# Block 1 of a gated cross-attention network: loads in parts, and products of weights inside the steps

## The chip, the cores and the metric

The kernel runs on one core of one Trainium2 chip. The metric is the device time of one execution in microseconds (us). TensorE (PE) multiplies matrices, VectorE (DVE) does elementwise work and reductions, ScalarE (ACT) exponentials and copies, GpSimd (POOL) some elementwise work and indirect transfers; SyncE (SP) issues most of the transfers.

## The reference, cut to what matters

Four blocks, each a gated cross-attention and a gated feed-forward part, work on x of 16 sequences by 128 tokens by 256 in float32. The change touches the first attention alone:

```
x = x + tanh(g_xattn[0]) * L0_xattn(layernorm(x), ctx, mask, Wq, Wk, Wv, Wo)

L0_xattn: 16 query heads, 8 key/value heads, head size 128
  q = (xn @ Wq)    k = (ctx @ Wk)    v = (ctx @ Wv)      # k, v repeated for two heads each
  attn = softmax(q k^T / sqrt(128), masked)
  out  = concat_heads(attn v) @ Wo
```

x is (16, 128, 256), ctx (16, 128, 128), Wq (256, 2048), Wk and Wv (128, 1024), Wo (2048, 256).

## The kernel before, in words

`Net.__init__` loads x in four parts of four sequences on SP's queue, and on ScalarE's queue the constants, the gates and the whole of the context in two layouts (`ctxT`, `ctx`, 1 MB each). The tiles stay in SBUF for the whole kernel.

`xattn0` never forms q, k and v. `products0` multiplies weights first. For each head h the query product is `wm[h] = Wq_h Wk_h^T / sqrt(128)` (256 by 128: two matmuls into a buffer of the PSUM tag `mm`, evicted by ScalarE, L578 and L581), and the value product is `wn[h] = Wv_h Wo_h` (128 by 256: one matmul into `mm`, evicted by ScalarE into the place of Wo's head, L562 and L563). Before the change all 16 query products and then all 16 value products come ahead of the steps. Four loads on SP's queue feed them: `wa` (WqT, 2 MB), `wc` (WkT, 0.5 MB), `wd` (WvT, 0.5 MB), `wb` (Wo, 2 MB).

The steps run over 64 units. `place(n)` takes a unit as a group g of four sequences (n // 16), a group of four heads hq (n // 4 % 4) and a sequence i of the group (n % 4). Step n issues, in the order of the text:

- `scores(n)`: four matmuls of `qT` with `ctxT` into PSUM tag `sc` (L620); VectorE adds the mask bias (s, L624), takes maxima (L527), subtracts them (e, L528); ScalarE takes the exponential (L531); VectorE sums and inverts (L538 to L542); GpSimd multiplies (L543)
- `queries(n // 4 + 1, n % 4)`: two matmuls of one head's `wm` with `xnT`, 512 columns wide, into `mm` (L609), copied to `qT` by ScalarE (L613). Four of them, one a step, make the next unit group's `qT`
- `turn(n - 1)`: four transposes (L516) and ScalarE's copy to `pT` (L518)
- `values(n - 2)`: one matmul with `ctx` (L634), ScalarE's copy to `aT` (L636)
- `project(n - 3)`: four matmuls with `wn` (L643), added to x by VectorE (L410)
- the layernorm of the next group of sequences, spread over a few steps (`norm_steps`: statistics at step 6, rows at 7 and 8, turns at 8 and 9 for the second group), and mask biases.

Ahead of step 0 come the layernorm of group 0, its mask bias and four `queries`. The order is written out by hand for TensorE, VectorE, ScalarE and GpSimd:

```python
with self.tc.manual_schedule(engines={ET.PE, ET.DVE, ET.Activation, ET.Pool}):
```

Inside it, each of these engines gets its instructions in the order of the program. SP is not in that list. PSUM tags have fixed numbers of buffers in this block: `sc` 2, `mm` 2, `tr` 2, `av` 1, `y` 1. At step 20 `empty_rows` starts filling buffers of the later routed parts with zeros on SP's queue. `ffn0` follows and loads its weights into `wa` and `wd` again, once their last readers are done.

Of the kernel before, what the change touches and what calls it, by code (L numbers as in the profile page):

```python
# [28 lines left out]
P = 128  # L29
B = 16  # L30
S = 128
D = 256
# [257 lines left out]
class Net:  # L290
    def __init__(self, tc, ctx, t, out):
        self.tc, self.nc, self.t, self.out = tc, tc.nc, t, out
        nc = self.nc
        self.const = ctx.enter_context(tc.tile_pool(name="const", bufs=1))
        self.wpool = ctx.enter_context(tc.tile_pool(name="wpool", bufs=1))
        self.small = ctx.enter_context(tc.tile_pool(name="small", bufs=4))
        self.dram = ctx.enter_context(tc.tile_pool(name="dram", bufs=1, space=DRAM))
        c = self.const
        self.n = 0

        self.x = c.tile([P, B, D], F32, name="x_sb")
        for g in range(4):
            nc.sync.dma_start(
                self.x[:, 4 * g : 4 * g + 4, :],
                t["x"][4 * g : 4 * g + 4].rearrange("b s h -> s b h"),
            )
        self.cst = c.tile([P, C_END], F32, name="cst")
        nc.scalar.dma_start(self.cst, t["cst"])
        self.ident = self.cst[:, C_ID : C_ID + P]
        gates = c.tile([P, 8], F32, name="gates")  # L310
        nc.scalar.dma_start(gates, t["gates"].partition_broadcast(P))
        self.rows, self.results = {}, {}
        self.head = self.routed = None

        self.mark = None
        self.ctxT = c.tile([P, B, S], F32, name="ctxT")
        nc.scalar.dma_start(self.ctxT, t["ctxT"])
        self.ctx = c.tile([P, B, S], F32, name="ctx")
        nc.scalar.dma_start(self.ctx, t["ctx"])
        self.xnT = c.tile([P, 2, NT], F32, name="xnT")  # L320
        self.nhalf = c.tile([P, 32], F32, name="nhalf")
        nc.gpsimd.memset(self.nhalf, -0.5)
        self.ones = c.tile([P, P], F32, name="ones")
        nc.gpsimd.memset(self.ones, 1.0)
        self.tg = c.tile([P, 8], F32, name="tg")
        nc.scalar.activation(self.tg, gates, AF.Tanh)

    def empty_rows(self, names, pool, after=None):

# [226 lines left out]

    def value_products(self, bank, wvT, wo, kv_of):

        nc = self.nc
        for h in range(16):  # L560
            pr = self.psum(bank, [P, D])
            nc.tensor.matmul(pr, wvT[:, kv_of(h), :], wo[:, h, :], start=True, stop=True)  # L562
            nc.scalar.copy(wo[:, h, :], pr)  # L563
        return wo


    def products0(self, pool):

        nc, t = self.nc, self.t
        wqT = self.weight("wa", t["L0_WqT"].rearrange("(h p) n -> p h n", p=P), [P, 16, D])  # L570
        wkT = self.weight("wc", t["L0_WkT"].rearrange("(h p) n -> p h n", p=P), [P, 8, P])
        wvT = self.weight("wd", t["L0_WvT"].rearrange("(h p) n -> p h n", p=P), [P, 8, P])
        wo = self.weight("wb", t["L0_Wo"].rearrange("(h p) n -> p h n", p=P), [P, 16, D])
        wm = self.sb(pool, "wm", [P, 2, 16, P], bufs=1)
        for h in range(16):
            pr = self.psum("mm", [P, 2, P])
            for kk in range(2):
                nc.tensor.matmul(  # L578
                    pr[:, kk, :], wqT[:, h, kk * P : (kk + 1) * P], wkT[:, h // 2, :], start=True, stop=True
                )  # L580
            nc.scalar.activation(wm[:, :, h, :], pr, AF.Copy, scale=1.0 / math.sqrt(128.0))  # L581
        return wm, self.value_products("mm", wvT, wo, lambda h: h // 2)

    def xattn0(self):
        nc, t = self.nc, self.t
        with self.tc.tile_pool(name="a0", bufs=2) as pool, self.tc.tile_pool(name="a0s", bufs=3) as sp:
            wm, wn = self.products0(pool)
            mraw = self.sb(pool, "mraw", [P, B, S], mybir.dt.uint8, bufs=1)
            nc.scalar.dma_start(mraw, t["mask"].partition_broadcast(P))
            some = self.sb(pool, "some", [P, B], bufs=1)  # L590
            nc.vector.tensor_reduce(some, mraw, AX.X, ALU.max)
            qT, mb, e, pT, aT = {}, {}, {}, {}, {}

            def place(n):

                return n // 16, n // 4 % 4, n % 4

            def mask(g):
                mb[g] = self.sb(pool, "mb", [P, 4, S])
                nc.vector.tensor_scalar(mb[g], mraw[:, 4 * g : 4 * g + 4, :], -NEG, NEG, ALU.mult, ALU.add)  # L600

            def queries(m, j):

                g, hq = divmod(m, 4)
                if j == 0:
                    qT[m] = self.sb(pool, "qT", [P, 4, 512])
                mm = self.psum("mm", [P, 512])
                for kk in range(2):
                    nc.tensor.matmul(  # L609
                        mm, wm[:, kk, 4 * hq + j, :], self.xnT[:, kk, g * 512 : (g + 1) * 512],  # L610
                        start=kk == 0, stop=kk == 1,
                    )
                nc.scalar.copy(qT[m][:, j, :], mm)  # L613

            def scores(n):
                g, hq, i = place(n)
                b = 4 * g + i
                sc = self.psum("sc", [P, 4, S])
                for j in range(4):
                    nc.tensor.matmul(  # L620
                        sc[:, j, :], qT[n // 4][:, j, i * S : (i + 1) * S], self.ctxT[:, b, :], start=True, stop=True
                    )
                s = self.sb(sp, "s", [P, 4, S], bufs=2)
                nc.vector.tensor_tensor(s, sc, mb[g][:, i : i + 1, :].to_broadcast([P, 4, S]), ALU.add)  # L624
                e[n] = self.exp_rows(sp, s, 1.0)
                self.normalise(e[n], some[:, b : b + 1])

            def turn(n):
                pT[n] = self.transpose4(sp, e.pop(n))

            def values(n):
                g, hq, i = place(n)
                o = self.psum("av", [P, 4, S])
                nc.tensor.matmul(o, self.ctx[:, 4 * g + i, :], pT.pop(n), start=True, stop=True)  # L634
                aT[n] = self.sb(sp, "aT", [P, 4, S])
                nc.scalar.copy(aT[n], o)  # L636

            def project(n):
                g, hq, i = place(n)
                y = self.psum("y", [P, D])  # L640
                a = aT.pop(n)
                for j in range(4):
                    nc.tensor.matmul(y, a[:, j, :], wn[:, 4 * hq + j, :], start=j == 0, stop=j == 3)  # L643
                self.add_to_x(4 * g + i, y, self.tg[:, 0:1])

            ET = mybir.EngineType
            N = 4 * B
            norm = self.norm_steps(sp, -6, 16)
            with self.tc.manual_schedule(engines={ET.PE, ET.DVE, ET.Activation, ET.Pool}):
                self.layernorm(sp, groups=(0,))  # L650
                mask(0)
                for j in range(4):
                    queries(0, j)
                for n in range(N + 3):
                    if n < N:
                        scores(n)
                    if n + 4 < N:
                        queries(n // 4 + 1, n % 4)
                    if 0 <= n - 1 < N:
                        turn(n - 1)  # L660
                    if 0 <= n - 2 < N:
                        values(n - 2)
                    if 0 <= n - 3 < N:
                        project(n - 3)
                    for f in norm.get(n, ()):
                        f()
                    if n % 16 == 8 and n + 8 < N:
                        mask(n // 16 + 1)
                    if n == 20:
                        self.empty_rows(("f1", "f2"), self.const, aT[n - 2].rearrange("p h s -> p (h s)"))  # L670
# [947 lines left out]
```

## Time and profile before

| | |
|---|---|
| median of 3 runs | 2532.65 us (2532.24 to 2535.24) |
| the profiled execution | 2590.16 us, span from first to last instruction 2588.1 us |
| mean granted TensorE clock | 0.916 of full; 1.00 in the first 400 us |
| TensorE busy in the span | 80% |
| VectorE, ScalarE, GpSimd busy | 58%, 34%, 31% |
| DMA | 299.33 MB, mean 116 GB/s; 274 GB/s in the first 50 us |
| block 1's attention | from the start to about 415 us |

Times in the profile are those of one execution, taken by the hardware profiler; it was longer than the runs that gave the median. A line of the order of time gives the start, the duration, the engine, the line of the code, the operation with the tiles it writes and reads, the number of merged instructions, and in brackets how long the engine had been idle before it and what ended the wait. Durations of matmuls are modelled at their ends: consecutive ones overlap, so the time that one takes on TensorE is read from start to start. PEld is TensorE's loading of the stationary operand, which overlaps with matmuls.

### The profile page before, as it was taken

Reading aid. Unit: us, or ns where it says so; the run is one execution under the profiler, and the core shown is the slowest. Engines: PE = TensorE matmul, PEld = TensorE weight load, DVE = VectorE, ACT = ScalarE, POOL = GpSimd, SP = SyncE. Lnnn points to the kernel's source line nnn. Section 1 sums busy time; section 2 is a strip of 40 time slices with the busy share of each in tenths; the row PEclk is TensorE's granted clock in tenths of the full one; section 3 lists DMA queues with packets and bytes.
Section 4 is the critical chain, followed back from the end, with each engine's and each line's share of the span. In section 5 each row is a group of like instructions: output and inputs, shape, how many; then the busy total and the mean of one; then the engine's idle time right before and its main releaser. Section 6 shows DMA issues by size and latency. Waiting matters only on the chain. (4 is left out here: it accounts for less than half of the span.)

```text
span 2588.1 us, 38336 instructions
## 1 busy us (share of the span) xinstructions
PE 2063.5 (80%) x13052; PEld 1423.3 (55%) x13052; DVE 1492.3 (58%) x4196; ACT 879.2 (34%) x1870; POOL 805.3 (31%) x799
## 2 busy tenths in 40 slices
PE   6999998788886878998989988988855878653770
PEld 3767764366664544665666654555534656532550
DVE  2766764478885445667666653454456755332448
ACT  3333333366662224444444431122213333201330
POOL 0221111243542222334444441122231134445340
PEclk9999998899997998999999999999987888766995
DMA  7049961119003760000000021388742001125768
GB/s 233 1 90 247 286 193 33 50 56 350 16 22 117 243 204 5 13 5 32 18 24 18 16 66 57 119 247 247 241 151 74 10 37 55 61 72 177 241 211 292
DMA packets 198567, 299.33 MB, mean 116 GB/s; under 512 B 21295, under 2 KB 151318, under 8 KB 195686
## 3 DMA queue, kind: packets, MB, share of 16 engines
q1 hardware_dynamic: 176102, 238.90, 31.9%
q0 software_dynamic: 19488, 55.31, 5.7%
q10 hardware_dynamic: 2784, 2.68, 0.3%
q8 instruction: 105, 1.72, 0.3%
q14 instruction: 88, 0.72, 0.1%
HBM read 160.92 MB, written 135.90 MB: 115 GB/s over the span
## 5 line engine op out<-in xcount | busy, mean ns | idle before, releaser
L273 POOL DMA_INDIRECT y_f<-ys,drow x182 | 174.1, 957 | 462.1 <-DVE ys L1039 248.4
L543 POOL TENSOR_TENSOR e<-e,r 128x512 f32<-128x512 f32 x128 | 132.7, 1037 | 585.3 <-DVE r L542 310.9
L240 POOL DMA_INDIRECT xs_f<-hx,hrow x224 | 221.4, 988 | 115.6 <-issue 57.3
L531 ACT ACTIVATE e<-e 128x512 f32<-128x512 f32 x128 | 80.7, 630 | 484.5 <-DVE e L528 484.5
L1017 PE MATMUL mm<-wgu,xeT 128*128 128x352 f32 x472 | 168.0, 479 | 7.2 <-DVE xeT L1010 2.9
L761 PE MATMUL tr<-cst,xe 128*128 128x128 f32 x364 | 73.3, 284 | 104.7 <-DMA xe<-xs_f 56.7
L1111 PE MATMUL qk<-wa,xnT 128*128 128x512 f32 x256 | 130.6, 634 | 23.8 <-DVE nq L1125 23.8
L538 DVE TENSOR_REDUCE sm<-e 128x4 f32<-128x512 f32 x128 | 87.8, 686 | 93.5 <-ACT e L531 92.7
L761 PEld LDWEIGHTS tr<-cst,xe 128*128 128x128 f32 x364 | 43.4, 143 | 157.7 <-issue 94.8
L1037 PE MATMUL o<-wdn,hT 88*128 88x256 f32 x472 | 123.5, 384 | 2.1 <-ACT hT L1030 2.1
L643 PE MATMUL y<-wb,aT 128*128 128x256 f32 x512 | 121.1, 379 | 1.0 <-DVE x_sb L410 1.0
L1164 PE MATMUL y<-wb,aT 128*128 128x256 f32 x512 | 120.9, 379 | 0.0
L1021 DVE TENSOR_TENSOR h<-sg,mm 128x176 f32<-128x176 f32 x118 | 39.7, 337 | 139.8 <-issue 89.8
L643 PEld LDWEIGHTS y<-wb,aT 128*128 128x128 f32 x512 | 97.1, 190 | 41.8 <-issue 18.7
L609 PE MATMUL mm<-xnT,wm 128*128 128x512 f32 x256 | 120.1, 593 | 0.0
L385 POOL TENSOR_TENSOR rr<-ss,nhalf 128x8 f32<-128x8 f32 x64 | 105.9, 1654 | 32.7 <-DVE ss L1119 32.6
L287 DVE TENSOR_TENSOR x_sb<-x_sb,yg 128x256 f32<-128x256 f32 x224 | 93.2, 423 | 31.0 <-DMA yg<-y_f 18.3
L1125 DVE TENSOR_TENSOR nq<-qk,rr 128x512 f32<-128x512 f32 x64 | 44.3, 692 | 113.1 <-POOL rr L385 113.1
L1030 ACT COPY hT<-tr 88x256 f32<-88x256 f32 x118 | 43.4, 368 | 190.9 <-PE tr L1028 190.8
L1017 PEld LDWEIGHTS mm<-wgu,xeT 128*128 128x128 f32 x472 | 82.3, 194 | 44.3 <-DVE xeT L1010 15.5
L839 DVE TENSOR_REDUCE mx<-sc 128x4 f32<-128x512 f32 x128 | 84.6, 682 | 37.3 <-PE sc L832 37.3
L516 PEld LDWEIGHTS tr<-cst,e 128*128 128x128 f32 x512 | 63.1, 141 | 72.2 <-issue 58.2
(288 smaller groups left out, 4909.6 us busy)
## 6 DMA issues: line engine op xcount, KB each, us to landing
wgu<-in_L_W SPq DMA_DIRECT2D x118, 352.0 KB
xs_f<-zeros SPq DMA_DIRECT2D x32, 1072.0 KB
wdn<-in_L_W SPq DMA_DIRECT2D x118, 176.0 KB
xs_f<-zeros SPq DMA_DIRECT2D x16, 1048.0 KB
y_f<-zeros SPq DMA_DIRECT2D x16, 1024.0 KB
yg<-y_f SPq DMA_DIRECT2D x16, 1024.0 KB
wgu<-in_L_gu SPq DMA_DIRECT2D x64, 192.0 KB
xe<-xs_f SPq DMA_DIRECT2D x79, 134.0 KB
```

Of the source, the lines that this page charges most:

```text
L240: ins = nc.gpsimd.indirect_dma_start(out=self.rows, out_offset=bass.IndirectOffsetOnAxis(ap=h["row"][:, j, k : k + 1], axis=0), in_=h["x"] ...
L273: self.net.unordered("y_" + self.name, self.net.nc.gpsimd.indirect_dma_start(out=self.y, out_offset=bass.IndirectOffsetOnAxis(ap=row, axis ...
L287: self.net.nc.vector.tensor_tensor(x, x, yg[:, k, :], ALU.add)
L385: return self.nc.gpsimd.tensor_tensor(out, var, self.nhalf[:, :n], ALU.pow)
L543: nc.gpsimd.tensor_tensor(e, e, r.unsqueeze(2).to_broadcast([P, 4, S]), ALU.mult)
L609: nc.tensor.matmul(mm, wm[:, kk, 4 * hq + j, :], self.xnT[:, kk, g * 512 : (g + 1) * 512], start=kk == 0, stop=kk == 1,)
L643: nc.tensor.matmul(y, a[:, j, :], wn[:, 4 * hq + j, :], start=j == 0, stop=j == 3)
L761: self.nc.tensor.transpose(tr[:, kk, :], src[:, kk * P : (kk + 1) * P], self.ident)
L1017: nc.tensor.matmul(gu, xeT[:, kk, :], wgu[:, kk, :], start=kk == 0, stop=kk == 1)
L1037: nc.tensor.matmul(y, hT[:, c, :], wdn[:, c, :], start=c == 0, stop=c == 1)
L1111: nc.tensor.matmul(q, self.xt(kk, b), wq[:, kk, cols], start=kk == 0, stop=kk == 1)
L1164: nc.tensor.matmul(y[b], a[:, j, :], wn[:, h, :], start=h == 0, stop=h == 15)
```

## The change

Loads: x's first part is issued in `__init__`, the other three behind the weights of their turn. The context's first four sequences are loaded at the start, the other twelve after the mask. The weights come in four parts of four heads, in the order WqT, WkT, WvT, Wo, on SP's queue. Products: four query products come ahead of the first `queries`; step n below 12 makes the query product of head n + 4 and step n below 16 the value product of head n, both between `scores(n)` and `queries`. The arithmetic is unchanged.

```diff
@@ Net.__init__
-        for g in range(4):
-            nc.sync.dma_start(
-                self.x[:, 4 * g : 4 * g + 4, :],
-                t["x"][4 * g : 4 * g + 4].rearrange("b s h -> s b h"),
-            )
+        self.load_x(0)
...
-        nc.scalar.dma_start(self.ctxT, t["ctxT"])
-        nc.scalar.dma_start(self.ctx, t["ctx"])
+        self.load_ctx(slice(0, 4))
...
+    def load_x(self, g):
+        self.nc.sync.dma_start(
+            self.x[:, 4 * g : 4 * g + 4, :],
+            self.t["x"][4 * g : 4 * g + 4].rearrange("b s h -> s b h"),
+        )
+
+    def load_ctx(self, some):
+        for dst, name in ((self.ctxT, "ctxT"), (self.ctx, "ctx")):
+            self.nc.scalar.dma_start(dst[:, some, :], self.t[name][:, some, :])
@@ value_products
+    def value_product(self, bank, wvT, wo, h):
+        pr = self.psum(bank, [P, D])
+        self.nc.tensor.matmul(pr, wvT, wo[:, h, :], start=True, stop=True)
+        self.nc.scalar.copy(wo[:, h, :], pr)
@@ products0
+        def load(dst, name, lo, n):
+            nc.sync.dma_start(
+                dst[:, lo : lo + n, :], t[name][lo * P : (lo + n) * P, :].rearrange("(h p) n -> p h n", p=P)
+            )
+
+        for g in range(4):
+            load(wqT, "L0_WqT", 4 * g, 4)
+            load(wkT, "L0_WkT", 2 * g, 2)
+            load(wvT, "L0_WvT", 2 * g, 2)
+            load(wo, "L0_Wo", 4 * g, 4)
+            if g in (1, 2, 3):
+                self.load_x(g)
-        for h in range(16):
+        def queries(h):
             pr = self.psum("mm", [P, 2, P])
             for kk in range(2):
                 nc.tensor.matmul(
                     pr[:, kk, :], wqT[:, h, kk * P : (kk + 1) * P], wkT[:, h // 2, :], start=True, stop=True
                 )
             nc.scalar.activation(wm[:, :, h, :], pr, AF.Copy, scale=1.0 / math.sqrt(128.0))
-        return wm, self.value_products("mm", wvT, wo, lambda h: h // 2)
+        def values(h):
+            self.value_product("mm", wvT[:, h // 2, :], wo, h)
+        return wm, wo, queries, values
@@ xattn0
+            wm, wn, query_product, value_product = self.products0(pool)
...
+            self.load_ctx(slice(4, B))
...
                 for j in range(4):
+                    query_product(j)
+                for j in range(4):
                     queries(0, j)
                 for n in range(N + 3):
                     if n < N:
                         scores(n)
+                    if n < 12:
+                        query_product(n + 4)
+                    if n < 16:
+                        value_product(n)
                     if n + 4 < N:
                         queries(n // 4 + 1, n % 4)
```

More of the change, by code (lines that the diff above doesn't have):

```diff
@@ L557, in value_products @@
     def value_products(self, bank, wvT, wo, kv_of):
-        nc = self.nc
         for h in range(16):
-            pr = self.psum(bank, [P, D])
-            nc.tensor.matmul(pr, wvT[:, kv_of(h), :], wo[:, h, :], start=True, stop=True)
-            nc.scalar.copy(wo[:, h, :], pr)
-        return wo
+            self.value_product(bank, wvT[:, kv_of(h), :], wo, h)
+        return wo
+    def value_product(self, bank, wvT, wo, h):
+        pr = self.psum(bank, [P, D])
+        self.nc.tensor.matmul(pr, wvT, wo[:, h, :], start=True, stop=True)
+        self.nc.scalar.copy(wo[:, h, :], pr)
     def products0(self, pool):
         nc, t = self.nc, self.t
[L570 to L573, printed above, removed]
+        wqT, wo = (self.sb(self.wpool, tag, [P, 16, D]) for tag in ("wa", "wb"))
+        wkT, wvT = (self.sb(self.wpool, tag, [P, 8, P]) for tag in ("wc", "wd"))
         wm = self.sb(pool, "wm", [P, 2, 16, P], bufs=1)
-        for h in range(16):
+        def load(dst, name, lo, n):
[10 more added lines that the diff above has]
+        def queries(h):
             pr = self.psum("mm", [P, 2, P])
@@ L586, in xattn0 @@
         with self.tc.tile_pool(name="a0", bufs=2) as pool, self.tc.tile_pool(name="a0s", bufs=3) as sp:
-            wm, wn = self.products0(pool)
+            wm, wn, query_product, value_product = self.products0(pool)
             mraw = self.sb(pool, "mraw", [P, B, S], mybir.dt.uint8, bufs=1)
             nc.scalar.dma_start(mraw, t["mask"].partition_broadcast(P))
+            self.load_ctx(slice(4, B))
             some = self.sb(pool, "some", [P, B], bufs=1)
```

## The prediction

> **What bounds the kernel now.** The change touches only block 1 (`xattn0`), so I read first the order of time of TensorE in the first 60 us. Columns: start, duration, engine, line, operation, tiles, count, and in brackets the idle time before it with its releaser.
>
> ```profile
> 9.26 1.97 PE L455 MATMUL tr<-cst,xn 128*128 128x128 f32 x8 [9.26 <-DVE xn L442]
> 25.44 11.41 PE L578 MATMUL mm<-wc,wa 128*128 128x128 f32 x64 [14.20 <-DMA wc<-in_L_WkT]
> 36.87 9.27 PE L562 MATMUL mm<-wb,wd 128*128 128x256 f32 x32
> 46.16 7.13 PE L609 MATMUL mm<-xnT,wm 128*128 128x512 f32 x16
> 53.13 1.33 PE L620 MATMUL sc<-ctxT,qT 128*128 128x128 f32 x8
> ```
>
> The start has four parts: 14.2 us of waiting for the load of `WkT`, which stands behind all of x and `WqT` in SP's queue; 11.4 us of query products; 9.3 us of value products; 7 us for the first four `queries`. The first `scores` starts at 53.13. (A float32 matmul of the code shows as two records.)
>
> Then one steady step, n = 11, in the same view, each engine by itself:
>
> ```profile
> 111.07 1.05 PE L620 MATMUL sc<-ctxT,qT 128*128 128x128 f32 x8
> 111.96 1.88 PE L609 MATMUL mm<-xnT,wm 128*128 128x512 f32 x4
> 113.68 0.60 PE L516 MATMUL tr<-cst,e 128*128 128x128 f32 x4
> 114.11 1.02 PE L634 MATMUL av<-pT,ctx 128*128 128x512 f32 x2
> 114.97 1.89 PE L643 MATMUL y<-wb,aT 128*128 128x256 f32 x8
> 116.70 1.05 PE L620 MATMUL sc<-ctxT,qT 128*128 128x128 f32 x8
> ...
> 112.16 0.69 DVE L624 TENSOR_TENSOR s<-sc,mb 128x512 f32<-128x512 f32 x1 [0.41 <-PE sc L620]
> 113.67 0.69 DVE L528 TENSOR_TENSOR e<-s,mx 128x512 f32<-128x512 f32 x1
> ...
> 114.40 0.63 ACT L531 ACTIVATE e<-e 128x512 f32<-128x512 f32 x1 [3.56 <-DVE e L528]
> 114.94 0.57 ACT L613 COPY qT<-mm 128x512 f32<-128x512 f32 x1
> 115.40 0.59 ACT L518 COPY pT<-tr 128x512 f32<-128x512 f32 x1
> ```
>
> TensorE has no idle bracket: it bounds the step, 116.70 − 111.07 = 5.63 us. Taken from start to start: scores 0.89, queries 1.72, turn 0.43, values 0.86, project 1.73. Now look at ScalarE. The `qT` copy needs only the queries, whose matmuls ended at 113.84, yet it ran at 114.94, after the exponential of the same step, which had waited 3.56 us for VectorE. **ScalarE takes its work in program order**, so whatever stands behind the exponential is 3.87 us late (114.94 − 111.07) against the start of the scores. Today nobody minds: a `qT` copy is read a group of steps later and `mm` has a second buffer.
>
> Last, what a pause costs TensorE, at a later place where it waits for a load: the order of time, then 2 us windows (busy us of PE, PEld, DVE, ACT, POOL; granted clock; DMA share; GB/s).
>
> ```profile
> 908.19 0.41 PE L761 MATMUL tr<-cst,xe 128*128 128x128 f32 x2 [1.87 <-DMA xe<-xs_f]
> ...
> 906.00:908.00 2.00, 0.32 (x2) 0.00 (x0) 0.34 (x1) 0.32 (x1) 0.66 (x1) 1.00 0.95 298
> 908.00:910.00 2.00, 1.81 (x6) 1.37 (x7) 0.92 (x4) 0.00 (x0) 0.00 (x0) 0.66 0.74 251
> 910.00:912.00 2.00, 2.00 (x6) 1.42 (x5) 0.48 (x1) 0.37 (x1) 0.96 (x1) 0.50 0.62 164
> ```
>
> A pause of 1.87 us halved the clock for about 4 us. I went through all pauses after 410 us with 1 us clock windows: of 11 near 2.0 us that began at full clock 8 were followed by half clock, of 4 near 2.5 us 3, of 15 longer ones all; of 25 near 1.5 us none.
>
> [...]
>
> **The change part by part.**
>
> *Loads in parts.* Ahead of the first query product stand now x's first part (0.5 MB), `WqT` for four heads (0.5), `WkT` for two (0.13) and on ScalarE's queue constants and four sequences of both contexts (0.8): 1.9 MB. In 3 us windows the DMA moved 86, 203 and 366 GB/s in the first 9 us, 2.0 MB in all; so they land at about 9 to 11 us[...]. That is when the layernorm of group 0, unchanged, leaves TensorE: 9.26 + 1.95 = 11.2 us. The 12 added issues on SP cost about 0.5 us each (x: four in 2.13) and hide behind transfers: SP's queue is held up by the transfers anyway (9.56 us on one issue before). ScalarE gets two more issues of about 0.5 us at 7.7 us, before its next work at 10.4: nothing. The mask is earlier, since it no longer stands behind 2 MB of context; its reduction (2.29) and bias (0.42) end before 20 us. Later parts: everything (9.5 MB) is in by about 31 us, as now (9.3 MB in the first 30), and head 12 is needed after 50 us: nothing.
>
> *New start.* Four query products[...] (0.85 us a head, the spacing of their evictions): 14.6 us. Four `queries`, 53.13 − 46.16 = 7.0[...]: first `scores` at 22.6 to 23. **Gain: 53.1 − 22.9 = 30.2 us.** Bounds: 26 if the weights land at 15 us[...].
>
> *Products in the steps, as matmuls.* A query product is 4 records of 128 columns at 0.89/8 = 0.111: 0.45. A value product is 2 records of 256 columns at 1.73/8 = 0.216: 0.43. TensorE is the bound, so 12 × 0.45 + 16 × 0.43 = 12.3 us.
>
> *The wait that comes in.* `queries(n//4+1, n%4)` reads `wm` of head n+4. For n below 12 that head's product is issued in the same step, right before, and its eviction stands on ScalarE behind the exponential of step n. So, from the start of scores: s at 1.09, e ends 3.33 (0.72 + 0.79 + 0.73 from start to start), eviction at 3.87, 0.38 long, queries at 4.30. Without the wait they would start at 0.89 + 0.88 = 1.77: **2.53 us of idle TensorE a step**. Behind the queries in TensorE's queue stand turn, values and project, so nothing fills it. A step is 4.30 + 1.72 + 0.43 + 0.86 + 1.73 = 9.04 us. Steps 0, 1, 2, where the pipeline fills: 6.0, 6.5, 7.3. Steps 0 to 11: 19.8 + 9 × 9.04 = 101.2.
> VectorE adds to it: the statistics of group 1 (step 6) and the rows (7, 8) run after the project's addition. Today its slack takes them; now they delay the next s: 2.3 us of statistics less the 1 us to the next scores' end, with the addition in front, about 1.9, then 1.4 and 1.3: 4.6 together. The four added transposes a step for two steps 0.9, as now. Sum 106.7, against 116.70 − 53.13 = 63.6: 43.1. Steps 12 to 15 carry a value product only, two `mm` uses on two buffers, no wait: 4 × 0.43 = 1.7. **Loss: 44.8 us**, the 12.3 included.
> The value products' evictions, behind the query product's, are done before `project` needs them (4.7 against 7.3 us in the step): nothing.
>
> *The clock.* The pause is 2.5 us in each of 12 steps, and above 4 in three. By the counts above some 7 to 8 in 10 halve the clock for about 4 us of continuous matmuls, which loses about 1.9 us: 12 × 0.7 × 1.9 = **16 us**; between 0 and 25.
>
> *What moves behind.* SP's loads of the next block's weights wait for the last reading of `wa` (step 11) and `wd` (step 15) instead of 37 and 46 us; they come at some 125 and 155 us, before the zero fills of step 20 in SP's queue and 250 us before their use: nothing. The fills move with step 20, by the net shift.
>
> *Sum.* −30.2 + 44.8 + 16 = +30.6 us. The profiled execution has a span of 2588.1 us (2590.16 as timed), 57.5 above the median of 2532.65; block 1 runs at clock 1.00 in it, so I carry the sum over unscaled: 2532.65 + 30 = about 2562 us.
>
> **Rivals.**
> *A, faster.* If ScalarE's evictions went ahead of the exponential, only the 12.3 us of matmuls would be paid: −18, 2515 us. For it: the products also fill TensorE's waits in steps 0 to 2 (some 3 us). Against it: the `qT` copy in its place behind the exponential. It decides from a stall of (30.2 − 12.3)/12 = 1.5 us a step downward.
> *B, wait without the clock.* −30.2 + 44.8 = +15: 2547 us. For it: three pauses of 1.8 to 2.0 us and one of 2.5 left the clock alone.
> *C, the parts don't help.* If the first product waited for the whole of its tile, the start would gain some 10 us only: 2532.65 + 51 = 2584. Against it: the statistics began at 5.13 us, when 0.7 MB had moved, less than the 2 MB of x; waits go by parts.
>
> **How the numbers follow.** Main forecast 0.60, B 0.20, A 0.12, a tie of gain and loss 0.03, C 0.05. About 0.2% (5 us) is what a measurement here can tell from no change. Faster 0.12, same 0.03, slower 0.85. Range: B less 7 us for the start, and the main sum with the clock lost nearly every time: 2540 to 2582; A, the tie and C lie outside.
>
> **What would show it.** First scores near 23 us (L620 by its new line); the evictions of `wm` after the exponential in every step below 12; TensorE idle there on ScalarE's `wm`, 2.5 us a time and longer in steps 7 to 9; a granted clock under 1 between 25 and 140 us; steps of 5.63 us from 16 on; block 1 ending some 30 us later than now. A step of 6.5 us in 3 to 11 would make it wrong.

## Result and the profile after

The changed kernel takes 2558.03 us (median of 4 runs, 2556.99 to 2566.12) against 2532.44 us of the kernel before (4 runs, 2528.75 to 2535.24): ratio 1.011, 95% interval 1.009 to 1.013. It is 25.6 us slower, and the forecast was 2562.

The two profiled executions can't be compared by their spans (2588.1 us before, 2554.8 after): the one of the kernel before was longer than each of the runs beside the changed kernel, as runs of it on one of the chips used below are too (2585 us). So I compare from the start of the kernel to the last step of block 1. The anchor is the VectorE instruction that takes up the scores of a step (`s`). For the last step, 63, before and after:

```profile
404.12 0.68 DVE L624 TENSOR_TENSOR s<-sc,mb 128x512 f32<-128x512 f32 x1
428.98 0.68 DVE L649 TENSOR_TENSOR s<-sc,mb 128x512 f32<-128x512 f32 x1
```

It starts 24.9 us later, which is the whole change within the interval of the times (23 to 33 us). From step 16 to step 63 the two executions take the same time, 263.8 us, so the change lies ahead of step 16.

**The start.** TensorE in order of time, after (start, duration, engine, line, operation, tiles, count, idle before and its releaser):

```profile
13.64 1.97 PE L460 MATMUL tr<-cst,xn 128*128 128x128 f32 x8 [13.64 <-DVE xn L447]
15.40 3.30 PE L598 MATMUL mm<-wc,wa 128*128 128x128 f32 x16
18.64 7.13 PE L634 MATMUL mm<-xnT,wm 128*128 128x512 f32 x16
25.61 1.33 PE L645 MATMUL sc<-ctxT,qT 128*128 128x128 f32 x8
```

The 14.2 us of waiting for weights are gone and so are the 17 us of products beyond the first four heads: first scores at 25.6 instead of 53.1. But the layernorm's transposes begin at 13.64, where before they began at 9.26. VectorE in order of time says why:

```profile
10.97 2.29 DVE L616 TENSOR_REDUCE some<-mraw 128x16 f32<-128x2048 uint8 x1 [3.24 <-DMA mraw<-in_mask]
13.18 1.60 DVE L447 TENSOR_SCALAR xn<-x_sb,mv,rs 128x256 f32<-128x256 f32 x4
```

The reduction over the mask, which is written outside the hand-made order, now stands ahead of the layernorm's rows (L447) and waits for its own load. Before, it stood behind them:

```profile
8.79 1.61 DVE L442 TENSOR_SCALAR xn<-x_sb,mv,rs 128x256 f32<-128x256 f32 x4 [1.23 <-POOL rs L385]
15.53 2.29 DVE L591 TENSOR_REDUCE some<-mraw 128x16 f32<-128x2048 uint8 x1 [5.12 <-DMA mraw<-in_mask]
```

**A step with the wait.** Step 3 after, TensorE and below it ScalarE:

```profile
45.73 1.05 PE L645 MATMUL sc<-ctxT,qT 128*128 128x128 f32 x8
46.62 0.61 PE L598 MATMUL mm<-wc,wa 128*128 128x128 f32 x4
47.07 0.60 PE L570 MATMUL mm<-wb,wd 128*128 128x256 f32 x2
50.02 1.98 PE L634 MATMUL mm<-xnT,wm 128*128 128x512 f32 x4 [2.36 <-ACT wm L601]
51.84 0.60 PE L521 MATMUL tr<-cst,e 128*128 128x128 f32 x4
52.28 1.02 PE L659 MATMUL av<-pT,ctx 128*128 128x512 f32 x2
53.14 1.89 PE L668 MATMUL y<-wb,aT 128*128 128x256 f32 x8
54.87 1.05 PE L645 MATMUL sc<-ctxT,qT 128*128 128x128 f32 x8
...
49.06 0.63 ACT L536 ACTIVATE e<-e 128x512 f32<-128x512 f32 x1 [2.55 <-DVE e L533]
49.60 0.37 ACT L601 ACTIVATE wm<-mm 128x256 f32<-128x256 f32 x1
```

The query product's matmuls are issued by 47.07, and their eviction (ScalarE's copy of the result out of PSUM, L601) waits until 49.60 behind the exponential. The queries (L634) start 4.29 us after the scores, right as that eviction ends, and the step takes 54.87 − 45.73 = 9.14 us. In the waits from 22 to 140 us (engine and line, what it waited for: total us, times, longest) it is the largest item of TensorE's matmuls:

```profile
PE mm L634 <- ACT wm L601: 30.0, 12, 4.2
```

Twelve times, once in each of steps 0 to 11: eleven pauses of 2.28 to 2.49 us and one of 4.19, in step 7. The clock, in the step after it (order of time, then 2 us windows: busy us of PE, PEld, DVE, ACT, POOL; granted clock, as a share of TensorE's full one; DMA share; GB/s):

```profile
59.15 3.68 PE L634 MATMUL mm<-xnT,wm 128*128 128x512 f32 x4 [2.35 <-ACT wm L601]
```

```profile
58.00:60.00 2.00, 0.85 (x1) 0.50 (x2) 1.24 (x4) 1.16 (x3) 0.00 (x0) 0.79 0.00 0
60.00:62.00 2.00, 2.00 (x4) 0.80 (x3) 0.02 (x1) 0.00 (x0) 1.04 (x1) 0.50 0.00 0
```

Here a pause of 2.35 us is followed by half clock (0.50), and the queries take 3.68 us instead of 1.98.

### The profile page after: what moved, and what is told of

It reads as the page before. It is cut to its first block, busy times and chain, and to the rows that moved or that the text cites. A ratio compares the mean times of both kernels' runs of the same rounds, so it can differ in the third digit from the quotient of the medians.

```text
span 2554.8 us, 38353 instructions
## 1 busy us (share of the span) xinstructions
PE 2038.9 (80%) x13052; PEld 1407.0 (55%) x13052; DVE 1490.9 (58%) x4196; ACT 880.5 (34%) x1870; POOL 807.5 (32%) x799
## 5 line engine op out<-in xcount | busy, mean ns | idle before, releaser
L634 PE MATMUL mm<-xnT,wm 128*128 128x512 f32 x256 | 129.3, 632 | 30.0 <-ACT wm L601 30.0
```

The costliest lines, as they stand in the source:

```text
L634: nc.tensor.matmul(mm, wm[:, kk, 4 * hq + j, :], self.xnT[:, kk, g * 512 : (g + 1) * 512], start=kk == 0, stop=kk == 1,)
```

## Experiments

Each kernel ran beside the kernel before on the same chip. On one chip, used for the third to the sixth row of the table, the kernel before took 2585.3 us; on another, used for the second row and the last three, 2532.79. So only ratios are compared across them. "Block 1" is the start of the last step's `s` against that of the kernel before, from the profiles.

| kernel | ratio to before, 95% interval | block 1, us |
|---|---|---|
| changed kernel | 1.011 (1.009 to 1.013) | +24.9 |
| changed kernel again | 1.009 (1.0064 to 1.0116) | +27.0 |
| both products ahead of scores | 0.9935 (0.9913 to 0.9957) | −14.9 |
| query product one head on | 1.0128 (1.0107 to 1.0148) | +22.8 |
| pause filled | 1.0052 (1.0035 to 1.0070) | +16.1 |
| loads alone | 0.9981 (0.9965 to 0.9997) | −3.9 |
| value product first | 1.0126 (1.0095 to 1.0156) | +36.4 |
| value product first, query product one head on | 0.9931 (0.9906 to 0.9956) | −15.1 |
| both ahead of scores, mask later | 0.9919 (0.9897 to 0.9941) | −18.3 |

### Both products ahead of scores

```diff
-                    if n < N:
-                        scores(n)
                     if n < 12:
                         query_product(n + 4)
                     if n < 16:
                         value_product(n)
+                    if n < N:
+                        scores(n)
```

> The changed kernel with both products of a step issued ahead of scores(n) instead of behind it, so that their evictions stand on ScalarE ahead of the exponential; no arithmetic is changed or left out. Wait theory: the pause of 2.3 to 2.5 us a step is gone; steps 3 to 11 take 5.63 + 0.88 = 6.5 us, the clock stays at 1.00 in block 1; against before the start gains 27.5 us and the products cost 12.3 us: about 2532 - 15 = 2517 us. Rival, the products or their evictions cost in themselves wherever they stand in the step: steps of about 9 us and 2558 us.

Measured: 2568.12 us against 2585.3, 17.2 us less, ratio 0.9935. TensorE and ScalarE, steps 4 and 5:

```profile
47.08 0.61 PE L598 MATMUL mm<-wc,wa 128*128 128x128 f32 x4
47.52 0.60 PE L570 MATMUL mm<-wb,wd 128*128 128x256 f32 x2
47.96 1.05 PE L645 MATMUL sc<-ctxT,qT 128*128 128x128 f32 x8
48.85 1.88 PE L634 MATMUL mm<-xnT,wm 128*128 128x512 f32 x4
53.59 0.61 PE L598 MATMUL mm<-wc,wa 128*128 128x128 f32 x4
...
47.72 0.38 ACT L601 ACTIVATE wm<-mm 128x256 f32<-128x256 f32 x1 [0.87 <-PE mm L598]
51.29 0.63 ACT L536 ACTIVATE e<-e 128x512 f32<-128x512 f32 x1 [2.76 <-DVE e L533]
```

The same matmuls and evictions, in another order: the evictions find ScalarE idle ahead of the exponential, the queries have no wait, a step takes 53.59 − 47.08 = 6.51 us, and the granted clock is 1.00 in each 1 us window up to 200 us, which is behind step 16. So the loss is the place of the products in the step, not the products.

### Which of two waits: a fresh head or a full buffer

The changed step gives the queries two reasons to wait for the same eviction: they read the head that it writes, and they are the third use of `mm` in the step, which has two buffers. Three kernels take one or both away.

Query product one head on:

```diff
-                for j in range(4):
+                for j in range(5):
                     query_product(j)
...
-                    if n < 12:
-                        query_product(n + 4)
+                    if n < 11:
+                        query_product(n + 5)
```

> The changed kernel with five query products ahead of the steps and step n making that of head n + 5: queries no longer reads a head made in its own step. Theory of two causes: the queries' PSUM buffer (third use of mm in the step, two buffers) is still the one whose eviction stands behind the exponential, so the pause and the step of 9.1 us stay: 2558 us within 6, the idle time put down to the same eviction. Rival, the reading of the fresh head alone makes the wait: pause gone, about 2518 us.

Measured: block 1 +22.8 us, ratio 1.0128. The head is no longer fresh, and the pause is the same, in step 3 as in the changed kernel:

```profile
48.04 0.60 PE L570 MATMUL mm<-wb,wd 128*128 128x256 f32 x2
50.99 1.98 PE L634 MATMUL mm<-xnT,wm 128*128 128x512 f32 x4 [2.35 <-ACT wm L601]
```

The buffer alone is enough. The median is 2617.06 us against 2585.3, 31.8 more and at the edge of what was expected (25.6 within 6), and 9 more than the block's shift. The profiled execution, of 2610.49 us, was the shortest of the four; the other three took 2616 to 2622, and what they had more is open.

Value product first (the product moved ahead of `scores(n)`, the query product of head n + 4 left behind it):

```diff
+                    if n < 16:
+                        value_product(n)
                     if n < N:
                         scores(n)
                     if n < 12:
                         query_product(n + 4)
-                    if n < 16:
-                        value_product(n)
```

> The changed kernel with only the value product moved ahead of scores(n); the query product of head n + 4 stays behind it. The step then has one eviction less behind the exponential and its queries find a PSUM buffer free, but they still read a head made in the same step. Theory that each of the two causes alone is enough: pause of 0.43 us more than in the changed kernel (about 2.8), steps of 9.13 + 0.34 = 9.5 us in 3 to 11, more half clock if anything: 4 to 12 us slower than the changed kernel, ratio to before 1.011 to 1.015. Rival, the buffer alone makes the wait: steps of 6.5 us, ratio 0.994.

Measured: ratio 1.0126, block 1 +36.4 us, 9.4 more than the changed kernel beside it. The buffer is free now and the head is fresh, and TensorE waits 2.79 us in step 3:

```profile
49.41 0.61 PE L598 MATMUL mm<-wc,wa 128*128 128x128 f32 x4
52.81 2.58 PE L634 MATMUL mm<-xnT,wm 128*128 128x512 f32 x4 [2.79 <-ACT wm L601]
```

The fresh head alone is enough as well. The whole comes out as expected, but the steps were longer than the 9.5 us expected (11.25 for steps 3 and 4), since half clock (0.50) came in eight places up to 160 us, for 3.4 us in five of them and for 6.8 in three.

Both edits at once:

> As the kernel with the value product first, and the query product one head on (n + 5, five heads ahead of the steps): neither the fresh head nor a full buffer stands in the way of queries, though the query product's eviction still stands behind the exponential. Wait theory: no pause, steps of 6.5 us in 3 to 11, clock 1.00, ratio 0.993 to 0.995. Rival, any eviction behind the exponential holds TensorE up: steps of 9 us, ratio 1.01.

Measured: ratio 0.9931, block 1 −15.1 us, steps 3 to 5 of 6.51 us, and the granted clock is 1.00 in each 1 us window up to 160 us, which is behind step 16. Step 4 on TensorE and ScalarE:

```profile
48.69 0.61 PE L598 MATMUL mm<-wc,wa 128*128 128x128 f32 x4
49.14 1.88 PE L634 MATMUL mm<-xnT,wm 128*128 128x512 f32 x4
...
51.13 0.63 ACT L536 ACTIVATE e<-e 128x512 f32<-128x512 f32 x1 [2.76 <-DVE e L533]
51.67 0.36 ACT L601 ACTIVATE wm<-mm 128x256 f32<-128x256 f32 x1
```

The eviction of the query product still stands behind the exponential (51.67), and the queries no longer wait for it (49.14, no bracket): they need neither its head nor its buffer in that step. Only in steps 1 and 2, which are shorter, does the value product wait for that buffer, 1.00 and 0.56 us.

### The clock

```diff
-        self.nc.tensor.matmul(pr, wvT, wo[:, h, :], start=True, stop=True)
+        for _ in range(times):
+            self.nc.tensor.matmul(pr, wvT, wo[:, h, :], start=True, stop=True)
...
-            self.value_product("mm", wvT[:, h // 2, :], wo, h)
+            self.value_product("mm", wvT[:, h // 2, :], wo, h, 6 if h < 12 else 1)
```

> The changed kernel with the value product's matmul issued six times over in steps 0 to 11 (each one overwrites the last), 5 x 0.43 = 2.15 us that fit into TensorE's pause of 2.3 us. Clock theory: the pauses are gone for the clock, not for the queries; no half clock before step 12, steps 3 to 6 all 9.1 us, steps 0 to 11 in about 107 us instead of 114: 2551 us. Rival, the half clock between 59 and 128 us costs nothing on the path: 2558 us. If the added matmuls don't fit, later than 2558.

Measured: 2600.42 us against 2585.3, ratio 1.0052; block 1 +16.1, 8.8 us earlier than in the changed kernel (10.9 against its second execution, below), although TensorE does 60 matmuls more. Step 4, then the 40 us window of this kernel and the same one of the changed kernel:

```profile
56.43 2.76 PE L571 MATMUL mm<-wb,wd 128*128 128x256 f32 x12
59.38 1.98 PE L635 MATMUL mm<-xnT,wm 128*128 128x512 f32 x4 [0.20 <-ACT wm L602]
```

```profile
65.00:105.00 40.00, 37.25 (x182) 27.74 (x181) 18.79 (x43) 11.89 (x25) 5.17 (x5) 1.00 0.00 1
```

```profile
65.00:105.00 40.00, 28.61 (x116) 18.93 (x116) 17.21 (x39) 9.84 (x21) 4.62 (x5) 0.85 0.00 1
```

With the pause filled, the queries start no earlier in the step, step 4 takes 9.13 us where the changed kernel took 10.82, and the granted clock is 1.00 in each 1 us window up to 200 us, though a pause of 2.03 us is left in step 7. So some 9 us of the loss are half clock; what remains of it, 16.1 us, is the wait, the products and the layernorm's delay less the earlier start.

### The loads alone

Here all 32 products stand ahead of the steps, as before, and only the loads come in parts.

> The changed kernel's loads in parts, with all 32 products ahead of the steps as before: the change without its moved products. Steps of 5.63 us; the first query product at 15.4 us instead of 25.4, the 20.7 us of products and 7 us of queries behind it, if the later weights don't hold it up: first scores at 43.5 instead of 53.1, a gain of about 10 us: 2523 us. If the later weights hold it up (all landed by 31 us, the value products need the last of them): gain of 5 to 10, up to 2528 us. Rival, the loads in parts are the loss: above 2532 us.

Measured: 2578.6 us against 2585.3, ratio 0.9981; block 1 −3.9 us, a little less than the 5 to 10 expected. TensorE at the start:

```profile
10.79 3.47 PE L598 MATMUL mm<-wc,wa 128*128 128x128 f32 x16 [10.79 <-DMA wc<-in_L_WkT]
14.10 1.33 PE L460 MATMUL tr<-cst,xn 128*128 128x128 f32 x8
16.80 2.63 PE L598 MATMUL mm<-wc,wa 128*128 128x128 f32 x16 [1.37 <-DMA wc<-in_L_WkT]
24.12 3.63 PE L598 MATMUL mm<-wc,wa 128*128 128x128 f32 x16 [4.69 <-DMA wc<-in_L_WkT]
29.54 3.08 PE L598 MATMUL mm<-wc,wa 128*128 128x128 f32 x16 [1.80 <-DMA wc<-in_L_WkT]
```

The first four heads are there at 10.8 us, but each further group comes behind Wo, the values and a part of x, so the last query products start at 29.5, and all 16 value products still stand behind them. With all 32 products ahead of the steps, in this order, the parts gain little; they pay together with products that are made later. An order of the 32 that takes up each group's value products as they land was not tried.

### Both products ahead of scores, mask later

To the first experiment's order this adds the mask's place:

```diff
-            nc.vector.tensor_reduce(some, mraw, AX.X, ALU.max)
...
                 self.layernorm(sp, groups=(0,))
+                nc.vector.tensor_reduce(some, mraw, AX.X, ALU.max)
                 mask(0)
```

> Both products ahead of scores(n), and the reduction over the mask put by hand behind the layernorm of group 0 on VectorE. In the changed kernel VectorE took it ahead of the layernorm's rows and waited 3.2 us for the mask, so that the transposes began at 13.6 instead of 9.3 us. Expected: transposes at 9.3 to 9.6, first scores 4 us earlier than with the products ahead alone (22.5 instead of 26.6 by TensorE), ratio 0.991 to 0.993. Rival, the first weights (landed by 10.8 us) or the mask's bias hold the start up: gain of under 2 us, ratio 0.9935.

Measured: 2512.72 us against 2532.79, ratio 0.9919. The start on VectorE and TensorE:

```profile
9.09 1.61 DVE L447 TENSOR_SCALAR xn<-x_sb,mv,rs 128x256 f32<-128x256 f32 x4 [1.23 <-POOL rs L390]
11.01 2.29 DVE L675 TENSOR_REDUCE some<-mraw 128x16 f32<-128x2048 uint8 x1 [0.31 <-DMA mraw<-in_mask]
...
9.56 1.97 PE L460 MATMUL tr<-cst,xn 128*128 128x128 f32 x8 [9.56 <-DVE xn L447]
23.19 1.05 PE L644 MATMUL sc<-ctxT,qT 128*128 128x128 f32 x8
```

Transposes at 9.56 as expected; the first scores come 3.4 us earlier than with the products ahead alone (26.59 there), not 4. This version beats both kernels: about 20 us faster than before and 46 faster than the changed one. Against the first experiment's order the gain of 3.4 us is plain in the profile and too small for the intervals of the times to separate.

### The changed kernel again

> The changed kernel itself once more beside the others, as their measure: ratio to before 1.009 to 1.013, block 1 ending 25 us later than before.

Measured: ratio 1.009, block 1 +27.0 us. Its steps 0 and 1 took 7.6 and 8.2 us instead of 6.0 and 6.5, since half clock came there already: the two executions of the same kernel have their half clock in different steps. The 2.1 us between their figures for block 1 show how much one profile of a kernel with such pauses can be off.

## Why the prediction was right, and where its terms were off

The forecast's +30.6 us stands against −27.5 + 52.4 = +24.9 in the profile. The mechanism was right: products behind the exponential make TensorE wait (2.28 to 2.49 us in eleven steps, 4.19 in one), the wait costs clock (0.50 in 5 stretches), and both together exceed the earlier start. That the total came within 4 us of 2562 is in part luck: the start gained 2.7 us less than forecast, while the clock cost 7 us less and the layernorm's delay 2.6 less. Point by point:

- **Start, −30.2: measured −27.5.** The weights' landing was right (9 to 11 us forecast, 10.79 in the loads-alone run). The failed step is "The mask is earlier … nothing": the earlier mask let its reduction slip ahead of the layernorm's rows on VectorE, 4.4 us on the transposes. The four query products and the queries then went 1.7 us faster than forecast. About 1 us of the forecast first scores (22.6 to 23, where 11.2 + 3.4 + 7.0 make 21.6) was an allowance of the author's that no measurement shows. The first three evictions of these products came 0.86 and 0.85 us apart, as forecast, and the fourth 0.53 behind the third (16.49, 17.35, 18.20, 18.73). The granted clock reads 1.00 in every 1 us window there, so a slow clock is not shown and the cause of the spacing stays open.
- **The wait: right, within 0.1 us a step.** Queries 4.30 us after the scores forecast, 4.29 measured; steps 0, 1, 2 of 6.0, 6.5, 7.3 forecast, 6.04, 6.48, 7.33 measured from `s` to `s`; later steps 9.04 forecast, 9.13 measured without half clock. What made it possible to forecast was one line of the profile before: the `qT` copy standing behind the exponential (at 114.94 us) though its input was ready (at 113.84). The forecast named only the fresh head, though, and counted the two `mm` buffers for steps 12 to 15 but not for 0 to 11; the runs showed a second sufficient cause, the third use of the two buffers. Both end at the same eviction, so the number did not suffer; for the query product one head on, the same argument would have forecast no pause.
- **Layernorm on VectorE, 4.6: about 2.** In the pause-filled run steps 6 to 9 exceed 9.13 us by 2.9 together, 0.9 of it the transposes. The statistics cost what was forecast (1.85 against 1.9), the rows nearly nothing instead of 2.7. Two of them took 1.38 us before and 0.72 to 0.73 after, see the last section.
- **The clock, 16: 8.8.** The mechanism was right, the frequency too high: 5 stretches of half clock in the 12 steps of one execution and 7 in the other, not 7 to 8 in 10 pauses as counted from later parts of the kernel. One costs about 1.7 us in a step (10.82 against 9.13), against 1.9.
- **Steps 12 to 15, 0.43 each: right** (6.06 and 6.07 against 5.63). **Behind block 1, nothing: right.** SP's loads for the next block came at 132 and 160 us (125 and 155 forecast), and the kernel's 25.6 us are the block's 24.9, as near as the times can tell.
- **Rivals.** A, the evictions ahead of the exponential, did not happen by itself but is what the first experiment built: −18 forecast, −17.2 measured. B, without the clock, was +15: the pause-filled run gives +16.1. C is out: the first product waits for its part alone (10.79).

## What to carry to other kernels

Before work is put into a step, look at what its eviction will stand behind in its engine's order (here ScalarE's copy at 49.60 us behind the exponential at 49.06, though its matmuls ended at 47.23), and who needs the result or the PSUM buffer in the same step; here the same change cost 25.6 us with its products behind the exponential and gained 17 with them ahead of it. Count the uses of a PSUM tag per step against its buffers, because moving the reading one step on helped nothing here while the buffer was still held (a pause of 2.35 us in step 3, 2.36 in the changed kernel). And an earlier load can move its consumer forward in an engine's order: an instruction outside a hand-made order may then wait ahead of the critical one (here the mask's reduction, which waited 3.24 us for its load, at 10.97 us, and the layernorm's rows behind it at 13.18 instead of 8.79).

## What the runs showed of the hardware that was not expected

VectorE's normalising of rows took longer where GpSimd had just begun a multiplication. Step 8 before, and below it the same rows after:

```profile
100.34 1.04 POOL L543 TENSOR_TENSOR e<-e,r 128x512 f32<-128x512 f32 x1 [4.61 <-DVE r L542]
100.47 1.38 DVE L442 TENSOR_SCALAR xn<-x_sb,mv,rs 128x256 f32<-128x256 f32 x2
...
110.62 0.72 DVE L447 TENSOR_SCALAR xn<-x_sb,mv,rs 128x256 f32<-128x256 f32 x2
```

Two rows took 1.38 us where they began 0.13 us after GpSimd, and 0.72 us with GpSimd idle. Before, all six such pairs of block 1 began 0.12 to 0.14 us after GpSimd and took 1.38; in the first experiment one began 0.82 us after it, with 0.22 us of GpSimd's work left, and took 0.73. Of GpSimd's 1.04 us 0.91 were left when the rows of step 8 began, and these took 0.66 us more than with GpSimd idle. No run here tested it by itself, so the cause stays open.

Of the eleven pauses of 2.2 to 2.5 us in each execution of the changed kernel, four were followed by half clock (0.50) in one and six in the other; with the one of 4.19 us it came in both. Each time it lasted 3.4 us, once 6.8 (by 1 us windows of the granted clock; from 59 us on 0.59, 0.50, 0.50, 0.70). Filling the pauses with useless matmuls made the kernel faster: block 1 came out at +16.1 us instead of +24.9.
